# Order of row fetches and of row copies in a graph network kernel: four plain fetches ahead of the first that adds, and later row copies behind the first two tiles'

## The chip, the cores and the metric

The kernel runs on one core of a Trainium2 chip. The metric is the device time of one execution in microseconds (us). The kernel before takes 3490.05 us, the median of three runs (3488.29 to 3501.34).

The core's engines work side by side and meet at semaphores: TensorE (PE, matrix products into PSUM), VectorE (DVE, elementwise work and reductions), ScalarE (ACT, copies and activations), GpSimd (POOL, which here issues the indirect fetches) and SyncE (SP, which issues the plain DMAs). Each has its own list of instructions in an order fixed when the program is built.

## The reference

64 graphs of 256 nodes with 256 features go through four layers. Layers 0, 1 and 3 are of one kind, with different weights; layer 2 is an attention layer over a node's neighbours. The first kind, with the adjacency matrix used twice:

```python
pre_u = jnp.einsum('bud,dk->buk', h_t, W1[:d])
pre_v = jnp.einsum('bvd,dk->bvk', h_t, W1[d:])
hidden = jax.nn.relu(pre_u[:, :, None, :] + pre_v[:, None, :, :] + b1)
S = jax.nn.sigmoid(jnp.einsum('buvk,ko->buvo', hidden, W2)[..., 0] + b2[0])
a_t = jnp.einsum('buv,bud->bvd', S * A_a, h_t)
m_t = jnp.einsum('uv,bud->bvd', A_m, h_t) * h_t
z_t = beta1 * h_t + beta2 * (jnp.einsum('bvd,de->bve', a_t, Wa) + ba) + beta3 * (jnp.einsum('bvd,de->bve', m_t, Wm) + bm)
```

The score S(u, v) counts only where the adjacency matrix is not zero, that is on few pairs (u, v), the edges; they are the same for all graphs.

## The kernel before

The kernel counts the edges, and since there are few it runs `few`. It computes scores on edges alone. The edges are laid out in tiles of 128, one edge per partition; a tile holds, for two graphs, the sum pre_u[u] + pre_v[v] of each of its edges as 2 x 256 numbers. VectorE then takes relu, multiplies by W2's row and sums (`rated`, which writes `junk` and a column of `raw`); ScalarE turns `raw` into `val`, VectorE multiplies it with the edges' weights into `rm`, and TensorE spreads these products over the matrix `sa` (`spread`, the matmuls `ps<-rm,gu`).

There are two ways to gather the sum of a tile:

- A tile "made" by TensorE (`made`, line 757): ScalarE copies 64 rows of `pre_u` and 64 rows of `pre_v` into the tile `pre` (`rows_u` and `rows_v`, lines 826 and 834), and one matmul with a 0/1 matrix `pick` gathers and adds them in PSUM (`ga<-pre,pick`). `rows_u` writes two tiles in one copy of 64x1024 numbers, `rows_v` one tile per copy of 64x512. The list `FAST` has eight such tiles, or six in some blocks.
- A "fetched" tile (`got`, line 776): `pre_u` and `pre_v` are also written to tables in DRAM (`tableu`, `tablev`, by SP). POOL fetches one row per partition from `tableu` by index, and then one from `tablev` with an add onto the same tile (`fetch`, line 807; the DMA is at line 820 in the profile). There are eight such tiles in a block, or ten (`more`), and a half tile `left` for the rest.

A block is one layer of this kind for two graphs; there are 96 blocks. A block with eight fetched tiles has 18 fetches, one with ten has 22; 64 and 32 blocks have them. Graphs run on two sides, "a" and "b", which alternate: while the scores of one side's layer are computed, the other side goes through its matrix work (`beside`, line 904, which steps through both by written lists of counts). A pass in which both sides take two graphs through all layers recurs 16 times.

The order of the work around the change:

- POOL's order is the list `FETCHES`, a pair (tile, 0) for the plain fetch from `tableu` and (tile, 1) for the one that adds from `tablev`; tile -1 is `left`. Each fetch is set behind the one before it with `tc.issue_after`. An add waits until the plain fetch of its tile has landed. The first `AHEAD` = 6 are issued as soon as the tables' first halves are written (in `before`, line 642), the rest from `scores` (line 695).
- On the other engines the order is made by a scheduler when the program is built, within what `issue_after` demands. In `before`, the row copies of tiles 0 and 1 are emitted last (`rows_v(st, 4 - 4 * m, 2, 0)` with m = 1); in `made` those of tiles 2 and 3 (n = 0), 4 and 5 (n = 1), 6 and 7 (n = 2), set behind `past[-1]`, the last `val` of the block before.

Of the kernel before, what the change touches and what calls it, by code (L numbers as in the profile page):

```python
# [35 lines left out]
MORE = FAST[6:]  # L36
FIRST = 4

FETCHES = [(0, 0), (1, 0), (2, 0), (0, 1), (3, 0), (1, 1)]
FETCHES += [(-1, 0), (2, 1), (4, 0), (3, 1), (-1, 1), (5, 0), (6, 0), (4, 1), (7, 0), (5, 1), (6, 1), (7, 1)]  # L40
FETCHES_MORE = FETCHES[:-2] + [(8, 0), (6, 1), (9, 0), (7, 1), (8, 1), (9, 1)]

# [20 lines left out]
def blk(c):  # L63
    return slice(c * P, (c + 1) * P)
# [37 lines left out]
def adj_seq_kernel(ctx: ExitStack, tc: tile.TileContext, a: dict, out: bass.AP):  # L102
# [15 lines left out]
    tensor, vector, scalar = Noting(nc.tensor), Noting(nc.vector), Noting(nc.scalar)  # L118
# [379 lines left out]
    def few(stack):  # L498
# [139 lines left out]
        def more(st, l):  # L638

            return (st["side"], l) in (("a", LAST), ("b", GNN[1]))  # L640

        def before(st, l):

            hT = st["hT"]
            pu = one.tile([P, 2, 2, D], FP, tag="pu" + st["side"], name="pu")
            pv = one.tile([P, 2, 2, D], FP, tag="pv" + st["side"], name="pv")
            pre = one.tile([P, len(FAST), 2 * D], FP, tag="pre" + st["side"], name="pre")
            order = [(m, g) for m in range(2) for g in range(2)]
            if l == LAST:
                order = [(m, g) for g in range(2) for m in range(2)]  # L650

            beside = {LAST: [0, (0, 1), (0, 1), (0, 1)], GNN[1]: [0] + [(0, 1)] * 3, GNN[0]: [0, 0, (0, 2), (0, 1)]}[l]
            beside = dict(zip(order, beside))
            st["tables"] = [
                tables.tile([N, 2 * D], FP, tag="table" + t + st["side"], name="table" + t) for t in "uv"
            ]

            st["pu"], st["pv"], st["pre"] = pu, pv, pre
            if l != GNN[1]:
                st["own"] = one.tile([P, 2, 2, D], FP, tag="own", name="own")  # L660
            t = one.tile([P, FIRST, 2, D], FP, tag="fetched" + st["side"], name="fetched")
            st["fetched"] = [t[:, f] for f in range(FIRST)]
            for m, g in order:
                if l == LAST and (m, g) == (1, 0):
                    st["flip"](1)
                t = psum()
                for c in range(2):
                    mm(out=t, lhsT=hT[:, c, g, blk(m)], rhs=w1[l][:, c], start=c == 0, stop=c == 1)
                scalar.copy(pu[:, m, g, :], t[:, 0, :])
                vector.tensor_tensor(pv[:, m, g, :], t[:, 1, :], b1row[l], ALU.add)  # L670
                if g == 1:
                    for rows, x in zip(st["tables"], (pu, pv)):
                        nc.sync.dma_start(out=rows[blk(m)], in_=flat(x)[:, m])
                    if m == 0:
                        st["fetches"] = list(FETCHES_MORE if more(st, l) else FETCHES)

                        if numbered:
                            fetch(st, AHEAD)
                if l != GNN[1]:
                    vector.tensor_tensor(st["own"][:, m, g, :], t[:, 0, :], pv[:, m, g, :], ALU.add)  # L680
                if g == 1:
                    if m == 0:
                        rows_u(st, 0, 2, 0, 0)
                    rows_v(st, 4 - 4 * m, 2, 0)
                yield beside[(m, g)]
                if l == GNN[1] and (m, g) == (0, 1):
                    st["turn"](0)
                    yield 0, 1
                    st["turn"](1)
                    yield 0  # L690
            yield REST_OF_IT

            yield from mixed(st, l, later if past else None, (0,) if more(st, l) else (0, 1))

        def scores(st, l, placed):
# [33 lines left out]
            def tile_scores(t, k, m, i):  # L729
                col = BLOCKS + 16 * m + 4 * k + i  # L730
                both(t, col, col + 8)
# [18 lines left out]
            def itself(m):  # L750

                with stay(vector):
                    if l == GNN[1]:
                        vector.tensor_tensor(*(flat(t)[:, m] for t in (own, st["pu"], st["pv"])), ALU.add)
                    both(own[:, m], DIAGONAL + 2 * m, DIAGONAL + 2 * m + 1)

            def made():
                for n, (k, m, i) in enumerate(fast):
                    t = ga.tile([P, 2, D], FP, tag="ga", name="ga")
                    with stay(tensor):  # L760
                        mm(out=t, lhsT=pick[:, k, 4 * m + i, :], rhs=pre[:, n], start=True, stop=True)
                    tile_scores(t, k, m, i)
                    if 2 * n + 2 < len(fast):

                        with tc.issue_after(past[-1]) if past else nullcontext():
                            rows_u(st, 2 * n + 2, 2, *FAST[2 * n + 2][:2])
                            if n != 1:
                                rows_v(st, 2 * n + 2, 2, FAST[2 * n + 2][0])
                    if n in (1, 2) and not placed:
                        itself(n - 1)  # L770
                    count.append(n)
                    yield
                    if n == 2 and more(st, l):
                        yield from mixed(st, l, None, (1,), ga)
# [25 lines left out]
            def end():  # L800
                rated_all(LATE, 1)
                past.append(st["rated"].ins)

            made = made()
            return made, got(made), end

        def fetch(st, n):

            now, st["fetches"] = st["fetches"][:n], st["fetches"][n:]
            for f, x in now:  # L810
                rows = st["tables"][x]
                if f < 0:
                    to, ids = st["left"], (left_u, left_v)[x]
                    rows = rows.rearrange("n (g d) -> (n g) d", g=2)
                else:
                    to, ids = st["fetched"][f].rearrange("p g d -> p (g d)"), (ids_u, ids_v)[x][:, f : f + 1]
                    if f < FIRST:
                        rows = rows[blk(0)]
                with tc.issue_after(fetches[-1]) if fetches else nullcontext():
                    this = nc.gpsimd.indirect_dma_start(  # L820
                        out=to, out_offset=None, in_=rows, in_offset=bass.IndirectOffsetOnAxis(ap=ids, axis=0),
                        compute_op=(ALU.bypass, ALU.add)[x],
                    )
                fetches.append(this.ins)

        def rows_u(st, f, n, k, m):

            h = halves[k]
            scalar.copy(
                st["pre"][h, f : f + n],  # L830
                st["pu"][h, m].rearrange("p g d -> p (g d)").unsqueeze(1).to_broadcast([64, n, 2 * D]),
            )

        def rows_v(st, f, n, k):

            for n in range(f, f + n):
                i = FAST[n][2]
                scalar.copy(
                    st["pre"][halves[1 - k], n], st["pv"][halves[i % 2], i // 2].rearrange("p g d -> p (g d)")
                )  # L840
# [37 lines left out]
        def stream(side, starts):  # L878

            sts = [{"b": b, "side": side} for b in starts]  # L880
            load(sts[0])
            short = [before(sts[0], GNN[0])]
            for i, st in enumerate(sts):
                yield short, (st, GNN[0]), False
                yield [after(st, GNN[0]), before(st, GNN[1])], (st, GNN[1]), True
                yield [after(st, GNN[1]), attention(st), before(st, GNN[2])], (st, GNN[2]), False
                short = [after(st, GNN[2])]
                if i + 1 < len(sts):
                    load(sts[i + 1])
                    short = [halfway(after(st, GNN[2]), 4, before(sts[i + 1], GNN[0]), 2)]  # L890
            yield short, None, False
# [29 lines left out]
        past, numbered, fetches, later = [], [], [], []  # L921
# [119 lines left out]
```

## Time and profile before

| | us |
|---|---|
| median of the runs (lowest, highest) | 3490.05 (3488.29, 3501.34) |
| the profiled execution | 3499.89 |
| its span, first to last instruction | 3498.2 |
| mean granted TensorE clock | 0.993 |
| ScalarE, a copy of `pre_u` rows, two tiles | 1.044 |
| ScalarE, a copy of `pre_v` rows, one tile | 0.617 |
| POOL, issue of a plain fetch, of an adding fetch (mean) | 1.010, 1.579 |
| VectorE, one `junk` of a tile and graph | 0.418 |

The profile is of one execution. Its page gives each engine's busy time and share of the span, the instructions grouped by source line, engine and tile, and the idle time ahead of a group with what ended it. "PE ga <- ACT pre" means that TensorE's matmul into `ga` waited for ScalarE's write of `pre`. Nearly all instructions of PE, DVE and ACT carry line 79, since a helper records them; they are told apart by their tiles. Queries of the trace answer with the waits of an engine, its instructions in order of time, and the busy time in chosen stretches.

### The profile page before, as it was taken

How to read it: one execution, taken by the hardware profiler on the slowest of the kernel's cores; microseconds unless marked ns; L12 is line 12 of the kernel's file. 1: busy time of each engine (PE TensorE's matmuls, PEld its weight loads, DVE VectorE, ACT ScalarE, POOL GpSimd, SP SyncE). 2: the span in 40 equal slices, each digit the busy share in tenths (PEclk: the TensorE clock that was granted, in tenths of full speed). 3: DMA queues.
4: the chain of work that ended last, by engine and by line, in shares of the span. 5: the costliest groups of instructions: out<-in, count | busy, mean ns of one | idle time of the engine just before them, and what ended most of it. 6: DMA issues, size and time to landing. Idle time of an engine off the chain costs nothing.

```text
span 3498.2 us, 48226 instructions
## 1 busy us (share of the span) xinstructions
PE 3391.1 (97%) x14200; PEld 2079.5 (59%) x14200; DVE 2626.2 (75%) x10526; ACT 1554.0 (44%) x2833; POOL 2409.6 (69%) x1882
## 2 busy tenths in 40 slices
PE   6999999999999999999999999999999999999998
PEld 3566565665656556565665656556565565656655
DVE  5777777777777777777777777777777777777776
ACT  2444444444444444544444444444444444444442
POOL 3767767677776767677677776776767667676765
PEclk7999999999999999999999999999999999999999
DMA  5788787877878878788787878778788788787875
GB/s 146 164 181 187 166 204 163 188 174 172 199 168 193 179 169 191 172 191 176 174 192 165 197 168 184 178 167 198 165 190 176 173 191 171 190 178 175 190 166 125
DMA packets 289070, 620.81 MB, mean 177 GB/s; under 512 B 39072, under 2 KB 56352, under 8 KB 288800
## 3 DMA queue, kind: packets, MB, share of 16 engines
q0 software_dynamic: 204800, 461.49, 66.6%
q1 hardware_dynamic: 82416, 154.96, 12.6%
q8 instruction: 115, 1.88, 0.2%
q10 hardware_dynamic: 1584, 1.20, 0.1%
q14 instruction: 155, 1.27, 0.1%
HBM read 500.06 MB, written 117.44 MB: 177 GB/s over the span
## 4 chain that ended last, share of the span: by engine, by line
PE 62%; POOL 10%; DMA 10%; DVE 8%; issue 7%; ACT 3%; another core or an unknown queue 0%; POOLq 0%; ACTq 0%; SPq 0%; DVEq 0%
PE ps L79 48%; PE ga L79 13%; POOL fetched L820 9%; DMA fetched<-tablev,ids_v 6%; DVE junk L79 3%; DMA fetched<-tableu,ids_u 3%; ACT pre L79 2%; DVE rm L79 1%; POOL left L820 1%; DVE sa L79 1%; DMA tableu<-pu 1%; DVE own L79 1%; ACT val L79 1%; ACT pu L79 1%; DVE mT L79 0%
## 5 line engine op out<-in xcount | busy, mean ns | idle before, releaser
L820 POOL DMA_INDIRECT fetched<-tablev,ids_v x832 | 1313.7, 1579 | 415.3 <-issue 256.1
L820 POOL DMA_INDIRECT fetched<-tableu,ids_u x832 | 840.5, 1010 | 548.8 <-DMA tableu<-pu 285.4
L79 DVE SCALAR_TENSOR_TENSOR junk<-fetched,L_gnn_w2row 128x256 f32<-128x256 f32 x1664 | 642.4, 418 | 205.8 <-DMA fetched<-tablev,ids_v 203.7
L79 PE MATMUL ga<-pre,pick 128*128 128x512 f32 x1408 | 721.5, 607 | 36.0 <-ACT pre L79 24.6
L79 PE MATMUL ps<-L_gnn_w,hT 128*128 128x512 f32 x1536 | 706.7, 597 | 5.8 <-DMA hT<-in_xT_dram 5.8
L79 DVE SCALAR_TENSOR_TENSOR junk<-ga,L_gnn_w2row 128x256 f32<-128x256 f32 x1408 | 537.3, 419 | 110.6 <-PE ga L79 94.6
L79 PEld LDWEIGHTS ps<-L_gnn_w,hT 128*128 128x128 f32 x1536 | 279.7, 190 | 323.2 <-issue 296.3
L79 ACT COPY pre<-pv 64x512 f32<-64x512 f32 x704 | 434.1, 617 | 70.8 <-DVE pv L79 47.3
L79 ACT COPY pre<-pu 64x1024 f32<-64x1024 f32 x352 | 361.4, 1044 | 7.4
L79 PE MATMUL ps<-sa,h 128*128 128x256 f32 x1536 | 359.8, 380 | 4.7 <-DVE sa L79 4.7
L79 PEld LDWEIGHTS ps<-sa,h 128*128 128x128 f32 x1536 | 291.7, 190 | 114.4 <-issue 62.5
L79 PEld LDWEIGHTS ga<-pre,pick 128*128 128x128 f32 x1408 | 248.5, 190 | 183.6 <-issue 92.5
L79 ACT COPY pu<-ps 128x256 f32<-128x256 f32 x384 | 142.8, 372 | 478.2 <-PE ps L79 450.3
L79 ACT ACTIVATE hb<-hT,L_gnn_zbias,scas 128x512 f32<-128x512 f32 x128 | 97.4, 807 | 479.3 <-DVE hT L79 368.1
L79 DVE TENSOR_TENSOR rm<-gva,val 128x256 f32<-128x256 f32 x768 | 279.8, 419 | 28.7 <-ACT val L79 21.2
L79 PE MATMUL ps<-adj,h 128*128 128x256 f32 x1280 | 296.8, 383 | 3.9 <-issue 3.9
L79 PEld LDWEIGHTS ps<-adj,h 128*128 128x128 f32 x1280 | 241.6, 191 | 74.1 <-issue 40.0
L79 DVE TENSOR_TENSOR pv<-ps,L_gnn_b1row 128x256 f32<-128x256 f32 x384 | 161.3, 420 | 135.5 <-ACT pu L79 128.8
L79 PEld LDWEIGHTS ps<-rm,gu 128*64 128x64 f32 x3072 | 174.7, 137 | 144.5 <-issue 54.1
L79 PE MATMUL ps<-rm,gu 128*64 128x128 f32 x3072 | 218.8, 280 | 32.6 <-DVE rm L79 31.0
L79 ACT COPY aT<-ps 128x512 f32<-128x512 f32 x192 | 112.4, 585 | 299.7 <-PE ps L79 267.5
L79 PE MATMUL ps<-mT,L_gnn_Wm 128*128 128x512 f32 x512 | 240.6, 592 | 0.0
(153 smaller groups left out, 4239.6 us busy)
## 6 DMA issues: line engine op xcount, KB each, us to landing
tableu<-pu SPq DMA_DIRECT2D x192, 256.0 KB
tablev<-pv SPq DMA_DIRECT2D x192, 256.0 KB
hT<-in_xT_dram SPq DMA_DIRECT2D x32, 512.0 KB
h<-in_x_dram SPq DMA_DIRECT2D x64, 256.0 KB
out_dram<-h SPq DMA_DIRECT2D x64, 256.0 KB
fetched<-tableu,ids_u POOLq DMA_INDIRECT x832
fetched<-tablev,ids_v POOLq DMA_INDIRECT x832
L_gnn_w<-in_L_gnn_W_dram SPq DMA_DIRECT2D x6, 256.0 KB
```

Of the source, the lines that this page charges most:

```text
L79: self.last = getattr(self.engine, op)(*a, **k)
L820: this = nc.gpsimd.indirect_dma_start(out=to, out_offset=None, in_=rows, in_offset=bass.IndirectOffsetOnAxis(ap=ids, axis=0), compute_op=( ...
```

## The change

Two things. In the list of fetches, the plain fetch of tile 3 moves ahead of the first fetch that adds. And the row copies of tiles 2 and later are, besides the wait for the block before, also set behind the last row copy that `before` emitted, which is `pre_v`'s for tile 1; before, the scheduler was free to put the `pre_u` copy of tiles 2 and 3 ahead of those, and did so in the blocks of the last layer.

```diff
-FETCHES = [(0, 0), (1, 0), (2, 0), (0, 1), (3, 0), (1, 1)]
+FETCHES = [(0, 0), (1, 0), (2, 0), (3, 0), (0, 1), (1, 1)]
 FETCHES += [(-1, 0), (2, 1), (4, 0), (3, 1), (-1, 1), (5, 0), (6, 0), (4, 1), (7, 0), (5, 1), (6, 1), (7, 1)]
...
                     if m == 0:
                         rows_u(st, 0, 2, 0, 0)
                     rows_v(st, 4 - 4 * m, 2, 0)
+                    st["rows"] = scalar.last.ins
                 yield beside[(m, g)]
...
                     if 2 * n + 2 < len(fast):
 
-                        with tc.issue_after(past[-1]) if past else nullcontext():
+                        with tc.issue_after(past[-1]) if past else nullcontext(), tc.issue_after(st["rows"]):
                             rows_u(st, 2 * n + 2, 2, *FAST[2 * n + 2][:2])
                             if n != 1:
                                 rows_v(st, 2 * n + 2, 2, FAST[2 * n + 2][0])
```

In the order as built, ScalarE's list differs in the two blocks of the last layer of each pass (32 in all), and at the start: `pre<-pv` twice, `pre<-pu`, `pre<-pv` twice, where it was `pre<-pu` and then `pre<-pv` four times. TensorE's list differs in one place of each pass: eight `rm` matmuls, `ga`, eight `rm`, `ga` becomes three `rm`, `ga`, thirteen `rm`, `ga`. There VectorE's first addition into `sa` moves behind the two `junk` of that `ga`. POOL's list differs in every block by the moved fetch.

## The prediction

> **What bounds the kernel now.** I read the page's busy shares first, then TensorE's waits, then the timeline round each kind of wait.
>
> ```profile
> PE 3391.1 (97%) x14200; PEld 2079.5 (59%) x14200; DVE 2626.2 (75%) x10526; ACT 1554.0 (44%) x2833; POOL 2409.6 (69%) x1882
> ...
> PE ps L79 <- DVE rm L79: 31.0, 33, 6.0
> PE ga L79 <- ACT pre L79: 24.6, 30, 1.3
> ...
> POOL fetched L820 <- DMA fetched<-tableu,ids_u: 165.6, 149, 3.3
> ```
>
> TensorE works nearly all the time, so nothing can gain more than its gaps: 102.9 us over the timeline, 35.6 of them in the first 100 us, 11.2 in the last 30, hence 56 in the steady part (columns: us in total, times, longest). The page's chain gives a quarter of the span to POOL and DMA, but TensorE works beside them; what counts is where the chain comes back to TensorE late. That is in two waits: `ga` matmuls for ScalarE's row copies, `ps<-rm,gu` for VectorE's products. The third line is what the fetch edit touches: POOL standing before an add until the rows it adds to have landed.
>
> The timeline (start us, us, engine, what, count, idle before and what ended it), ScalarE and then TensorE, at the last layer of one side, and TensorE at that of the other:
>
> ```profile
> 1904.93 0.22 ACT L79 ACTIVATE val<-val 128x16 f32<-128x16 f32 x1
> 1905.17 1.04 ACT L79 COPY pre<-pu 64x1024 f32<-64x1024 f32 x1
> 1906.23 2.53 ACT L79 COPY pre<-pv 64x512 f32<-64x512 f32 x4
> ...
> 1904.80 1.09 PE L79 MATMUL ps<-rm,gu 128*64 128x128 f32 x16
> 1906.90 1.12 PE L79 MATMUL ga<-pre,pick 128*128 128x512 f32 x2 [1.01 <-ACT pre L79]
> 1907.96 1.09 PE L79 MATMUL ps<-rm,gu 128*64 128x128 f32 x16
> 1908.98 1.13 PE L79 MATMUL ga<-pre,pick 128*128 128x512 f32 x2
> ...
> 1949.59 1.12 PE L79 MATMUL ga<-pre,pick 128*128 128x512 f32 x2 [0.72 <-ACT pre L79]
> ```
>
> ScalarE copies `pre_u` rows of tiles 2 and 3 (1.04 us) and only then tile 0's own `pre_v` row, for which TensorE idles. Both places recur 16 times, once per pass of 213 us.
>
> POOL, VectorE, TensorE and (share of the 16 DMA engines, the last column but one) the stretch in which POOL waits:
>
> ```profile
> 2227.22 0.95 POOL L820 DMA_INDIRECT fetched<-tableu,ids_u  x1 [0.30 <-issue]
> 2231.37 1.81 POOL L820 DMA_INDIRECT fetched<-tablev,ids_v  x1 [3.20 <-DMA fetched<-tableu,ids_u]
> 2233.48 0.98 POOL L820 DMA_INDIRECT fetched<-tableu,ids_u  x1 [0.30 <-issue]
> ...
> 2229.91 0.43 DVE L79 SCALAR_TENSOR_TENSOR junk<-fetched,L_gnn_w2row 128x256 f32<-128x256 f32 x1 [1.56 <-DMA fetched<-tablev,ids_v]
> ...
> 2232.46 0.78 PE L79 MATMUL ps<-rm,gu 128*64 128x128 f32 x6 [2.09 <-DVE rm L79]
> ...
> 2228.40:2230.40 2.00, 1.98 (x19) 0.97 (x17) 0.49 (x3) 0.00 (x0) 0.00 (x0) 1.00 0.86 311
> 2230.40:2232.40 2.00, 0.00 (x0) 0.00 (x0) 1.38 (x6) 1.60 (x4) 1.03 (x1) 1.00 0.08 31
> ```
>
> While POOL waits, the DMA engines run dry (0.08). The VectorE line belongs to the block before, whose first add waited 2.95 us: its last add lands late, VectorE idles 1.56 us, then `rm`, and TensorE 2.09 us.
>
> [...] POOL's 3.20 us hold up every later fetch. [...]
>
> **Part 1, ScalarE, first place (16 times).** No instruction is added; the copy `pre<-pu` of tiles 2 and 3 moves behind the two `pre<-pv` of tiles 0 and 1. Tile 0's row then runs from 1905.17 (VectorE finished its source `pv` at 1905.02) to 1905.79; TensorE starts 0.05 later, as now: 1905.84 for 1906.90, 1.06 earlier. But the compiled order also moves this `ga`: it now stands behind 3 instead of 8 `rm` matmuls, with 13 instead of 8 behind it. Five of 0.107 us each (start to start in the timeline; a matmul has two records, so x16 is eight) come after it, 0.53. Net 1.06 − 0.53 = 0.53, times 16 = **8.5 us**. The second eight need `rm` products done at 1906.94, before TensorE reaches them at about 1907.4: hidden. VectorE's first `sa` addition moves behind two `junk` of tile 0; I get the second `sa` done at 1909.26, TensorE asking at 1909.4: hidden by 0.14 us, and at worst the 0.53 is lost. Tiles 2 and 3 are complete at the same time as now.
>
> **Part 1, second place (16 times).** Same swap, TensorE's order unchanged. The 16 waits (0.31 to 1.30, three of them put to "issue") sum to 8.5 us; each but one (1.30) is under the 1.04 us by which the copy comes earlier. Gain 8.5 − 0.3 = **8.2 us**. TensorE next meets `rm`, of which the later half is done at 1949.62 and wanted at about 1950: hidden, narrowly.
>
> **Part 2, POOL.** Before the first add there are now four plain fetches. The fourth passes that add; its 0.98 us plus 0.30 issue fill the wait. Per block POOL gains the smaller of 1.28 and the add's wait in excess of 0.30. Over the 96 blocks that wait averages 1.70 us in the 64 blocks with 18 fetches and 1.20 in the 32 with 22, so 0.91 us per block, and 1.26 in the 33 that start without a pause. Everything after the second add is issued that much sooner, over the whole block. The second add needs tile 1's rows, issued 1.28 after tile 0's: no new wait. The reused semaphore for which the moved fetch now waits is of a DMA eight issues back, some 12 us, against 5 to 8 us from issue to use where VectorE waits: hidden.
>
> Where does it reach TensorE? 23 of its waits on `rm` (19.2 us) follow VectorE's wait for a landed add by under 9 us. Taking for each the smaller of the wait and its block's POOL gain, I get 13.6 us; the last block adds 1.26 at the end, where TensorE waits 6.0 us: **14.9 us**. The other `rm` waits, mostly 0.43 us behind an activation, stay.
>
> Its unknown: the first add is issued 1.28 minus the excess later where the excess is smaller (up to 0.6 in most long blocks, those with 22 fetches), and its data follow one more fetch. A fetch costs the engines 66.6% of 3498.2 us over 1664 + 96 full fetches = 1.32 us; so it lands 0 to 1.9 later. I take 1. VectorE waits for tile 0 at once only in long blocks, and there it waits again about 2.5 us for tile 1, which comes sooner: hidden.
>
> **Sum.** 8.5 + 8.2 + 14.9 = 31.6. The gains overlap: what TensorE saves at the second place makes it earlier at the next `rm` wait, whose fetches started before. I take 85%, **27 us**. The profiled execution, 3499.89 us (span 3498.2), would be 3473; it lies 9.8 over the median 3490.05, so 3463 for the median.
>
> **Rivals.**
> A: ScalarE's part alone pays, the fetches being hidden or held by the DMA engines, which are 0.9 to 1.0 busy late in many blocks. For it: adds' data queue there. Against: the dry 2 us. 8.5 + 8.2 = 17, so 3473.
> B: almost nothing: `ga` behind three `rm` costs its gain, VectorE (75% busy overall, all of some 5 us stretches) is late instead. 0 to 8 us, say 3486.
> C, slower: the first add lands too late. It decides once the delay exceeds the 2.5 us that VectorE idles before tile 1 in the 32 long blocks; each us beyond costs up to 32. With part 2's gain gone, it needs 17/32 = 0.5 us more to end slower at all; two adds in a row that cost 4 us of delay would give 3490 − 17 + 1.5 × 32 = 3521. Against it: my bound is 1.9, and adds already follow each other three in a row at each block's end, where they are used 5 to 8 us after issue.
> That the change does nothing is out: the compiled order shows both moves.
>
> **Numbers.** Both parts 0.57 (3444 to 3471), A 0.20, B 0.14, C 0.09. 0.5% of 3490, 17.5 us, is about what a measurement of this kernel can tell. A lies on that bound and is halved: faster 0.57 + 0.10 = 0.67; same 0.10 + 0.14 = 0.24; slower 0.09. Range: 3445 (45 of the steady 56 us of gaps, should waits that I didn't count close too) to 3487 (B), leaving out C and the tails.
>
> **What would show it.** `PE ga <- ACT pre` falls from 24.6 to under 10 us, at the first place about 0.55 per wait; POOL's `fetched <- DMA fetched<-tableu` from 165.6 to about 80; `PE ps <- DVE rm` from 31 to about 17. Wrong if VectorE's wait for `tablev` (203.7 us) grows, if `ps<-sa,h` starts to wait, or if POOL's gain only lengthens its wait for the tables.

## The result, and the profile after

The changed kernel took 3602.56 us, the median of four runs (3596.70 to 3612.65), against 3491.45 for the kernel before beside it: a ratio of 1.0318, with a 95% interval of 1.0293 to 1.0342. It is slower by 111 us where 27 us less had been forecast. The profiled execution took 3603.28 us, its span 3601.6. Measured again with other runs beside it, the same program was once 2.0% slower and twice 0.9% faster; that is the main finding, and the experiments below turn on it.

The page of the kernel after, busy time of each engine:

```profile
PE 3441.3 (96%) x14200; PEld 2102.7 (58%) x14200; DVE 2622.5 (73%) x10526; ACT 1551.6 (43%) x2833; POOL 2416.4 (67%) x1882
```

TensorE does the same 14200 matmul records, but is busy 50.2 us longer and idle 53.2 us longer (span less busy: 160.3 against 107.1). The waits of the kernel after (who waits for what: us in total, times, longest):

```profile
POOL fetched L821 <- DMA tableu<-pu: 485.4, 68, 12.9
...
PE ps L79 <- DVE sa L79: 88.7, 46, 3.3
...
POOL fetched L821 <- DMA fetched<-tableu,ids_u: 56.1, 56, 3.0
...
DVE junk L79 <- DMA fetched<-tablev,ids_v: 36.7, 41, 2.3
...
PE ps L79 <- issue: 17.0, 17, 3.0
...
PE ps L79 <- DVE rm L79: 10.7, 10, 7.0
...
PE ga L79 <- ACT pre L79: 6.4, 16, 0.4
```

Everything that the change aimed at has fallen: POOL's wait for the rows it adds to from 165.6 to 56.1 us, VectorE's wait for landed adds from 203.7 to 36.7, TensorE's waits for `rm` from 31.0 to 10.7 and for ScalarE's copies from 24.6 to 6.4. Part of the fall comes from TensorE being later with everything else: in a profile of the same program at 3470 us, shown further below, these four waits are 122.0, 171.4, 26.4 and 6.7 us. In their place stand two others. POOL waits 485.4 us for the tables, 286.0 before; with VectorE's wait for landed adds down to 36.7 us, that is not what holds TensorE up. And TensorE's matmuls `ps<-sa,h` wait for VectorE's additions into `sa`; before, that was 4.7 us in five waits.

Where it happens is seen in the timeline of the kernel after, at the first place (last layer of side a; start us, us, engine, what, count, idle before and what ended it). ScalarE, TensorE, VectorE and POOL, one after the other:

```profile
642.62 1.04 ACT L79 COPY pre<-pu 64x1024 f32<-64x1024 f32 x1
643.66 1.25 ACT L79 COPY pre<-pv 64x512 f32<-64x512 f32 x2
...
642.12 1.12 PE L79 MATMUL ga<-pre,pick 128*128 128x512 f32 x2 [0.39 <-ACT pre L79]
643.18 1.74 PE L79 MATMUL ps<-rm,gu 128*64 128x128 f32 x26
644.85 1.12 PE L79 MATMUL ga<-pre,pick 128*128 128x512 f32 x2
645.81 0.59 PE L79 MATMUL ps<-sa,h 128*128 128x256 f32 x2
649.12 1.65 PE L79 MATMUL ps<-sa,h 128*128 128x256 f32 x5 [2.71 <-DVE sa L79]
...
644.08 0.69 DVE L79 TENSOR_TENSOR sa<-sa,ps 128x512 f32<-128x512 f32 x1
648.38 0.69 DVE L79 TENSOR_TENSOR sa<-sa,ps 128x512 f32<-128x512 f32 x1 [3.61 <-remote]
...
643.03 1.01 POOL L821 DMA_INDIRECT fetched<-tableu,ids_u  x1 [0.30 <-issue]
644.35 0.94 POOL L821 DMA_INDIRECT fetched<-tableu,ids_u  x1 [0.30 <-issue]
645.59 1.56 POOL L821 DMA_INDIRECT fetched<-tablev,ids_v  x1 [0.30 <-issue]
```

The edits have done their work. ScalarE's copies of tiles 2 and 3 now follow those of tiles 0 and 1, `ga` waits 0.39 us where it waited 1.01, and POOL goes from its fourth plain fetch into the first add with 0.30 us between. Then: the last of the thirteen `rm` matmuls ends, by its record, at 643.18 + 1.74 = 644.92. VectorE has nothing else to do and stands before its second addition into `sa`, which needs those matmuls and nothing more. It starts at 648.38, 3.46 us later; the trace names no releaser ("remote"). Meanwhile TensorE has run into `ps<-sa,h`: the first matmul needs only the first half of `sa`, the second needs the other half and waits 2.71 us for it. VectorE waits for TensorE's report, and TensorE for VectorE.

"Report" is here the semaphore event by which VectorE learns that the matmuls are done. The trace has the end of the matmul's record and, 3.46 us later, the start of the addition, and names no releaser; so it can't tell whether the matmul ended late or only its report came late. On another occasion (run e3_after below) the same addition of the same program starts 0.04 us behind that end, as the next timeline shows, TensorE and VectorE at the same place of the same pass:

```profile
625.89 1.74 PE L79 MATMUL ps<-rm,gu 128*64 128x128 f32 x26
627.56 1.13 PE L79 MATMUL ga<-pre,pick 128*128 128x512 f32 x2
628.52 2.75 PE L79 MATMUL ps<-sa,h 128*128 128x256 f32 x12
...
626.79 0.69 DVE L79 TENSOR_TENSOR sa<-sa,ps 128x512 f32<-128x512 f32 x1
627.67 0.69 DVE L79 TENSOR_TENSOR sa<-sa,ps 128x512 f32<-128x512 f32 x1 [0.19 <-PE ps L79]
```

With the start of `rm` as zero, the first addition comes at 0.90 us in both. The second comes at 1.78 us here and at 5.20 us there. Nothing in the program differs.

A late report costs twice, which the windows of the kernel after show (us of the stretch, then busy time and count of PE, PEld, DVE, ACT and POOL, the granted TensorE clock, the share of the DMA engines, GB/s):

```profile
646.00:648.00 2.00, 0.41 (x2) 0.00 (x1) 0.00 (x0) 0.00 (x0) 1.57 (x2) 1.00 0.58 174
...
650.00:652.00 2.00, 2.00 (x7) 1.55 (x6) 1.73 (x11) 0.59 (x1) 1.70 (x2) 0.51 0.82 152
```

First TensorE, VectorE and ScalarE stand still. Then TensorE works at half clock: from 650.03 on, 0.91 us behind the end of the 2.71 us wait, the granted clock is 0.50 for 3.41 us, and the records of `ps<-sa,h` start 0.43 us apart instead of 0.22. Of the 42 gaps of TensorE over 1.5 us behind the first 100 us of this profile, 24 have a half-clock stretch that begins between the start of the gap and 3.5 us behind its end, the shortest of these gaps being 1.56 us long; the other 18, of 1.55 to 3.18 us, have none. The changed kernel has 28 half-clock stretches here and 8 in e3_after, at mean granted clocks of 0.982 and 0.991.

The two spans of this one program, 3601.6 and 3470.4 us, differ by 131.2. TensorE's idle time is 160.3 against 73.9, 86.4 more: its waits `ps<-sa,h` for VectorE are 88.7 against none, those put to "issue" 17.0 against 3.5, and those for `rm` 10.7 against 26.4, so 88.7 + 13.5 − 15.7 = 86.5. Its busy time is 3441.3 against 3396.5, 44.8 more. The clock's loss, estimated from the mean granted clocks as (1 − 0.982) × 3601.6 = 64.8 against (1 − 0.991) × 3470.4 = 31.2, accounts for about 34 of that; what makes up the other 11 stays open.

### The profile page after: what moved, and what is told of

It reads as the page before. It is cut to its first block, busy times and chain, and to the rows that moved or that the text cites. A ratio compares the mean times of both kernels' runs of the same rounds, so it can differ in the third digit from the quotient of the medians.

```text
span 3601.6 us, 48226 instructions
## 1 busy us (share of the span) xinstructions
PE 3441.3 (96%) x14200; PEld 2102.7 (58%) x14200; DVE 2622.5 (73%) x10526; ACT 1551.6 (43%) x2833; POOL 2416.4 (67%) x1882
## 4 chain that ended last, share of the span: by engine, by line
PE 86%; DVE 5%; another core or an unknown queue 2%; ACT 2%; issue 2%; POOL 1%; DMA 0%; POOLq 0%; DVEq 0%; ACTq 0%
PE ps L79 69%; PE ga L79 17%; DVE junk L79 2%; DVE sa L79 2%; ACT pre L79 1%; DVE rm L79 1%; POOL fetched L821 1%; ACT val L79 0%; ACT pu L79 0%; DMA fetched<-tablev,ids_v 0%; DVE own L79 0%; DVE pv L79 0%; DMA fetched<-tableu,ids_u 0%; ACT logits L79 0%
## 5 line engine op out<-in xcount | busy, mean ns | idle before, releaser
L79 DVE SCALAR_TENSOR_TENSOR junk<-fetched,L_gnn_w2row 128x256 f32<-128x256 f32 x1664 | 638.3, 418 | 37.1 <-DMA fetched<-tablev,ids_v 36.7
L79 PE MATMUL ps<-sa,h 128*128 128x256 f32 x1536 | 407.7, 410 | 99.9 <-DVE sa L79 88.7
L79 PEld LDWEIGHTS ps<-sa,h 128*128 128x128 f32 x1536 | 310.2, 205 | 241.9 <-DVE sa L79 118.6
L79 DVE TENSOR_TENSOR rm<-gva,val 128x256 f32<-128x256 f32 x768 | 279.9, 419 | 28.2 <-ACT val L79 15.7
L79 DVE TENSOR_TENSOR hT<-hb,ps 128x512 f32<-128x512 f32 x128 | 87.9, 687 | 241.4 <-PE ps L79 241.3
L79 DVE TENSOR_TENSOR sa<-sa,ps 128x512 f32<-128x512 f32 x192 | 129.4, 684 | 182.8 <-remote 89.7
```

The lines of the kernel that those rows point to most:

```text
L79: self.last = getattr(self.engine, op)(*a, **k)
```

## Experiments

All medians are in us. The ratio is the record's own estimate from the single runs, and differs from the ratio of the medians by up to 0.0014. "Late" counts, of the 96 second additions into `sa` (one per block), those which start more than 1.5 us after the recorded end of their last `rm` matmul.

| run | what | median | before beside it | ratio (95%) | late | `ps<-sa,h` for VectorE |
|---|---|---|---|---|---|---|
| first | change | 3602.56 | 3491.45 | 1.0318 (1.0293–1.0342) | 51 | 88.7 |
| e1_fetch | fetch order alone | 3478.10 | 3495.73 | 0.9953 (0.9936–0.9969) | 0 | 0 |
| e1_rows | ScalarE's order alone | 3493.31 | 3495.73 | 0.9998 (0.9988–1.0008) | 0 | 0 |
| e1_two | two plain fetches ahead | 3585.81 | 3495.73 | 1.0257 (1.0240–1.0275) | 0 | 0 |
| e1_paced | fetch order, paced | 3508.59 | 3495.73 | 1.0035 (1.0017–1.0053) | 0 | 0 |
| e2_after | change | 3569.10 | 3496.48 | 1.0200 (1.0174–1.0227) | 49 | 85.5 |
| e2_before | before | 3494.08 | 3496.48 | – | 3 | 2.9 |
| e2_rows_a | change, rows on side a only | 3565.50 | 3496.48 | 1.0211 (1.0182–1.0240) | 45 | 63.9 |
| e2_rows_b | change, rows on side b only | 3565.67 | 3496.48 | 1.0186 (1.0160–1.0212) | 49 | 78.5 |
| e3_after | change | 3467.98 | 3496.74 | 0.9912 (0.9894–0.9930) | 0 | 0 |
| e3_fetch | fetch order alone | 3478.99 | 3496.74 | 0.9948 (0.9931–0.9965) | 0 | 0 |
| e3_rows | ScalarE's order alone | 3495.67 | 3496.74 | 0.9992 (0.9982–1.0002) | 0 | 0 |
| e3_paced | fetch order, paced | 3509.72 | 3496.74 | 1.0035 (1.0020–1.0051) | 0 | 0 |
| e4_both_paced | change, paced | 3507.25 | 3503.50 | 1.0012 (1.0003–1.0021) | 1 | 0 |
| e4_rows | ScalarE's order alone | 3501.35 | 3503.50 | 1.0000 (0.9987–1.0013) | 11 | 11.8 |
| e5_fetch | fetch order alone | 3475.87 | 3495.27 | 0.9937 (0.9918–0.9956) | 0 | 0 |
| e5_after | change | 3469.11 | 3495.27 | 0.9913 (0.9894–0.9933) | 0 | 0 |
| e5_mend | change, more work before `sa` | 3543.04 | 3495.27 | 1.0132 (1.0109–1.0154) | 0 | 0 |
| e6_fetch | fetch order alone | 3601.63 | 3503.74 | 1.0267 (1.0233–1.0300) | 50 | 81.5 |

Runs whose names begin alike (e1, e2, ...) were measured on one chip, side by side. The groups fall into two kinds. In e1, e3 and e5 no report is late, whatever the kernel. In the first measurement, e2, e4 and e6 some are late; in the first measurement and e2 that holds for the kernel before too (four and three), in e4 and e6 it was not profiled. The first kind I call prompt, the second late. All profiles of the kernel before are of late occasions. Where waits of a prompt run are set against its waits below, the two occasions differ as well; its own two profiles have 31.0 and 26.3 us for `rm`, 24.6 and 22.6 for `pre`.

### Which part costs: the first group

The first trace suggested theory 1: plain fetches that follow one another closely delay TensorE's reports. Theory 2 put the cost down to ScalarE's part, which moves a `ga` and VectorE's additions; theory 3 was the prediction's rival C, the first add landing late.

```diff
 # e1_fetch: the kernel before, with the new list
+FETCHES = [(0, 0), (1, 0), (2, 0), (3, 0), (0, 1), (1, 1)]
```

> The fetch order alone, ScalarE's copies as before. Theory 1 (three or four plain fetches in a row delay the moment at which TensorE's finished rm matmuls are reported to VectorE; VectorE's second addition into sa is late, TensorE stands before ps<-sa,h and then works at half clock): 3560 to 3620 us, TensorE's wait ps<-sa,h for VectorE 60 us or more, against 4.7 before. Theory 2 (the cost comes from ScalarE's part: three rm, ga, thirteen rm at the first place): 3470 to 3490 us, that wait under 10 us. Theory 3 (the first add lands late): VectorE's wait for tablev over 204 us.

```diff
 # e1_rows: the change, with the old list
+FETCHES = [(0, 0), (1, 0), (2, 0), (0, 1), (3, 0), (1, 1)]
```

> ScalarE's order alone, the fetches as before. Theory 1: 3465 to 3485 us, the wait ps<-sa,h under 15 us, ga for ScalarE's pre under 10 us. Theory 2: 3580 to 3610 us, with the wait ps<-sa,h once per pass at the first place at least.

```diff
 # e1_two: the kernel before, two plain fetches ahead of the first add
+FETCHES = [(0, 0), (1, 0), (0, 1), (2, 0), (1, 1), (3, 0)]
```

> The kernel before with two plain fetches ahead of the first add instead of three: (0,0) (1,0) (0,1) (2,0) (1,1) (3,0). Theory 1: the late reports become rarer than before (the wait ps<-sa,h at most 5 us, no addition into sa later than 1 us after its last rm matmul while VectorE idles), POOL waits longer for the rows it adds to (165.6 us to 250 or more), the time 3490 to 3530 us. Theories 2 and 3: no view on the wait; the time by POOL alone, the same range.

```diff
 # e1_paced: e1_fetch, and in fetch() ahead of the issue
+                if (f, x) == (3, 0):
+                    for _ in range(2):
+                        with tc.issue_after(fetches[-1]):
+                            fetches.append(nc.gpsimd.memset(st["fetched"][3], 0.0).ins)
```

> The fetch order of the changed kernel alone, but POOL is kept busy about 1.3 us ahead of the fourth plain fetch (it clears that tile twice, which the fetch overwrites). Theory 1, by the rate of the plain fetches: the wait ps<-sa,h falls to under 25 us and the time to 3490 to 3530 us. If what counts is only that four plain fetches stand ahead of the first add, at whatever rate, it stays at 3560 to 3620 us with 60 us or more.

None of them explains the 111 us from here: neither part alone was slower, and no addition was late in any of the four. The waits of e1_fetch, then of e1_rows:

```profile
PE ga L79 <- ACT pre L79: 24.7, 32, 1.9
...
PE ps L79 <- DVE rm L79: 16.6, 23, 6.0
```

```profile
PE ps L79 <- DVE rm L79: 43.9, 43, 5.7
...
PE ga L79 <- ACT pre L79: 7.0, 16, 0.7
```

The fetch order alone gains 17.6 us by the medians, and the wait for `rm` falls by 14.4. ScalarE's order alone takes 17.6 us from the wait for `pre`, and the wait for `rm` grows by 12.9: nothing is left. e1_two shows how much hangs on what stands ahead of the first add: with two, three and four plain fetches the kernel takes 3586, 3496 and 3478 us. The waits of e1_two:

```profile
PE ps L79 <- DVE rm L79: 87.5, 50, 5.8
PE ga L79 <- ACT pre L79: 40.4, 40, 1.8
```

I had expected 3490 to 3530 from POOL's longer wait (it rose to 341.9 us). TensorE's two waits grew by 56.5 and 15.8 us, and its mean clock fell to 0.983 (0.993 in the first profile of the kernel before). The pause of e1_paced costs 13 us against the kernel before, where the same order without it gains 17.6.

Two new theories stood then: the parts hurt only together (theory 4), or what was slow in the first measurement is a property of the occasion (theory 5).

### Only together, or only sometimes: the second and third groups

e2_after and e2_before are the changed kernel and the kernel before, with no edit.

> The changed kernel once more, beside the kernels of this group. Theory 4 (the two parts hurt only together): 3580 to 3615 us, ps<-sa,h waiting for VectorE 60 us or more, and the second addition into sa over 2.5 us behind its last rm matmul in most passes, as in its first profile. Theory 5 (the late reports are not a property of the program, but of the occasion on which it was measured): 3455 to 3490 us, that wait under 10 us and the second addition 0.1 us behind.

> The kernel before, profiled beside them. Its first profile had four waits ps<-sa,h of 0.5 to 1.8 us, each behind a late report of an rm matmul. Theory 5: none of these here, and a span 3 to 10 us shorter. Theory 4: a few again, at the same places of other passes.

```diff
 # e2_rows_a, and e2_rows_b with "b"
-... tc.issue_after(st["rows"]):
+... tc.issue_after(st["rows"]) if st["side"] == "a" else nullcontext():
```

> The new fetch order, with ScalarE's new order only in the last layer of side a (the first place, where TensorE's list becomes three rm, ga, thirteen rm). Theory 4: slower than the fetch order alone (3478) if the hurt comes from TensorE's moved ga, 3530 to 3600; 3470 to 3485 if it comes from the second place. Theory 5: 3465 to 3480 us.

> The new fetch order, with ScalarE's new order only in the last layer of side b (the second place, where TensorE's list is as before). Theory 4: the reverse of the run with side a, 3530 to 3600 if the hurt comes from here, else 3465 to 3480. Theory 5: 3465 to 3480 us.

The change was slow again, and with ScalarE's part in only one of the two places it was as slow. That looked like theory 4, but the kernel before had late reports too, three of 96, where the four kernels of the first group, so near to it, had none. So the third group put the change and its parts side by side; e3_fetch, e3_rows and e3_paced are the kernels of the first group, e3_after is the changed kernel.

> The changed kernel in one group with its two parts alone. On a chip like that of the first group (all of TensorE's reports prompt, none of its semaphore events missing from the trace), theory 5 expects 3455 to 3480 us and no wait ps<-sa,h; theory 4 (the parts hurt only together) 3560 to 3615 on any chip. On a chip like that of the second group both expect 3560 to 3615.

> The fetch order alone. Theory 4: 3470 to 3485 us on any chip. Theory 5 with theory 1 (on some chips TensorE's reports are late while plain fetches follow one another closely): 3470 to 3485 on a chip with prompt reports; 3550 to 3610 on one with late reports, with ps<-sa,h waiting 50 us or more and 40 or more of the 96 second additions into sa over 1.5 us late.

> ScalarE's order alone. Theory 4: 3485 to 3500 us on any chip. Theory 5 with theory 1: the same on a chip with prompt reports; on one with late reports 3485 to 3510, with a few late additions as in the kernel before (under 15 over 1.5 us), because its fetches are as before.

> The new fetch order with about 1.3 us of POOL work ahead of the fourth plain fetch, ScalarE as before: 3508.6 us and no late report in the first group. Theory 4: again 3500 to 3520. Theory 5 with theory 1: again so on a chip with prompt reports; on one with late reports between the kernel before and the fetch order alone, under 25 second additions over 1.5 us late, since the fetches are further apart.

Theory 4 fell: the program that took 3603 us takes 3468, and no report is late. Each of its parts does what it did in the first group. The two kinds of occasion can be told apart without looking at any addition. On late ones semaphore events are missing from the trace: of the 11984 updates by TensorE, VectorE and ScalarE of the changed kernel 9882 are there, against 11983 in e3_after. In all nine late profiles 82 to 87% are there, in all eleven prompt ones at least 99.9%. It is not the chip alone: groups e1 and e4 ran on the same one. What the occasions differ in stays open. One suspect was not tested: every time here comes with a recorded span, and the missing events are missing from that recording, so no run shows whether the late reports would come without it.

### What makes a report late: the other groups

In seven late profiles of either fetch order (the first two, the four of e2, and e6_fetch), I took the share of the 16 DMA engines that packets of plain fetches held from 0.2 us before to 0.8 us after the end of each block's last `rm` matmul. Under 0.4, 20 of 364 second additions are over 1 us late; from 0.4 up, 254 of 308. Packets of adding fetches go the other way: in the first two profiles 58 of 133 additions are over 1 us late where these packets held under 0.4, and 1 of 59 from 0.4 up. In ten prompt profiles (all but e5_mend) 460 of 960 additions fall into the upper class too, and none is late.

The pooled count hides that the two orders differ. In the upper class 245 of 252 are late with the new fetch order, but 9 of 56 with the old one. So a high share of plain packets does not make a report late by itself. A pause of POOL separates the cases better. Take for each addition the block whose fetches began last before the end of its `rm`, and POOL's longest pause ahead of that block's first add. In the two profiles of the kernel before, 12 of 27 additions without a pause over 0.6 us are over 1 us late, and none of 165 with one. In e4_rows, with the same fetch order, it is 12 of 14, and 1 of 82; in the five late profiles of the new order 262 of 409, and none of 71. So it shows within one and the same program. And the fourth plain fetch fills just this pause: in the first measurement 84 of 96 blocks have it in the kernel before, 12 in the changed one. On prompt occasions none of 462 additions without it is late. All of that is correlation; the next runs put a pause back.

e4_both_paced is the changed kernel with the four lines of e1_paced, e4_rows is e1_rows.

> Both parts of the change, with about 1.3 us of POOL work ahead of the fourth plain fetch. On a chip with late reports: if the plain fetches that follow one another closely cause them, under 30 of the 96 second additions into sa are over 1.5 us late (49 and 51 in the changed kernel there) and the time is 3500 to 3550 us; if ScalarE's part or the mere order causes them, 45 or more and 3565 to 3610. On a chip with prompt reports: none late, 3490 to 3510 us.

> ScalarE's part alone, fetches as before. On a chip with late reports: under 15 second additions over 1.5 us late and 3485 to 3510 us if the plain fetches cause them; 40 or more and 3550 or more if ScalarE's part does. On a chip with prompt reports: none, 3485 to 3500 us, as twice before.

The occasion was of the late kind (10264 of 11984 events in e4_rows). With a pause ahead of the fourth plain fetch one addition is late instead of 51 or 49 (seven more are 1.1 to 1.4 us late), and the line `ps<-sa,h` for VectorE is gone from TensorE's waits. TensorE, VectorE and POOL at the first place, in the same pass as above:

```profile
631.27 1.74 PE L79 MATMUL ps<-rm,gu 128*64 128x128 f32 x26
...
633.05 0.69 DVE L79 TENSOR_TENSOR sa<-sa,ps 128x512 f32<-128x512 f32 x1 [0.19 <-PE ps L79]
...
631.13 1.01 POOL L825 DMA_INDIRECT fetched<-tableu,ids_u  x1 [0.30 <-issue]
632.14 1.12 POOL L823 MEMSET fetched<- 128x512 f32 x2
633.53 0.95 POOL L825 DMA_INDIRECT fetched<-tableu,ids_u  x1 [0.27 <-POOL fetched L823]
```

The second addition starts 0.04 us behind the end of `rm` (631.27 + 1.74 = 633.01). With the fetches as before and ScalarE's part alone there are 11 late additions, and the time is that of the kernel before. So ScalarE's part is not the cause; the fetch order without a pause is what brings the late reports, so far as one run with the pause shows. The changed kernel itself was not run on this occasion (its 51 and 49 are from two others), and the pause also moves the fourth fetch and all behind it later, so that spacing and moment are not told apart.

e5_fetch and e5_after are again the fetch order alone and the change.

> The fetch order alone, beside the whole change. With late reports on this occasion: 3545 to 3600 us and 40 or more of the 96 second additions over 1.5 us late, if the closely following plain fetches are the cause by themselves; under 20 and 3475 to 3510 if ScalarE's part is needed too. With prompt reports: 3470 to 3490 us, as twice before.

> The whole change again. With late reports: 3560 to 3610 us, 45 or more late. With prompt reports: 3460 to 3480 us, none late.

```diff
 # e5_mend: the change, and at the end of spread()
-            yield 1 if l == GNN[1] else 2
+            yield 3 if l == GNN[1] else 4
```

> The whole change, with two more of the made tiles stepped between the rm matmuls and ps<-sa,h, so that TensorE has 0.4 to 1.7 us more of other work before it needs the second addition. With late reports: the reports stay as late (40 or more over 1.5 us), but the wait ps<-sa,h falls from 85 us to 50 or less and the time to 3510 to 3560 us. With prompt reports: no wait to save, 3465 to 3500 us, by whether the earlier tiles find their row copies done.

This occasion was prompt, so the mend had no late report to hide. It missed its range: moving the tiles forward made other matmuls wait (47.2 us for ScalarE's `logits`, which cost 0.2 in e5_after) and lost 74 us against the change. Whether more work between `rm` and `sa` would pay on a late occasion was not seen. The last run is the fetch order alone once more.

> The fetch order alone, on another occasion. With late reports: 3545 to 3600 us and 40 or more of the 96 second additions over 1.5 us late, if the closely following plain fetches are the cause by themselves; under 20 and 3475 to 3510 us if ScalarE's part is needed too. With prompt reports: 3470 to 3490 us, as on three occasions before, and nothing is told apart.

This time the occasion was late. The waits of e6_fetch:

```profile
PE ps L79 <- DVE sa L79: 81.5, 57, 3.5
PE ga L79 <- ACT pre L79: 17.3, 19, 1.0
```

The fetch order alone, 0.5 to 0.6% faster on three prompt occasions, costs 2.7% here, as much as the whole change in its first measurement. The new fetch order is enough by itself to bring the late reports on such an occasion; a pause in it took nearly all of them away in the one run that tried. No kernel here beats the kernel before on both kinds of occasion: on prompt ones the change is the best, on late ones nothing gains.

## Why the prediction was right or wrong

**Part 2, POOL, 14.9 us: near in size on prompt occasions.** The fetch order alone gains 17.6, 17.8 and 19.4 us there, and TensorE's waits for `rm` are 16.6 to 20.7 us, against 31.0 in the profile before. POOL's wait for the rows it adds to is 113.0 us in e1_fetch, not about 80, and most of what it saves there it waits longer for the tables (326.7 us against 286.0). Landed adds still come sooner: VectorE waits 157.2 us for them, 203.7 before.

**Part 1, ScalarE, 8.5 + 8.2 us: the waits right, the gain wrong by itself.** `ga` for `pre` fell to about 7 us in e1_rows, e3_rows, e3_after and e5_after, and the first place waits 0.39 us in the timeline shown, near the 0.53 to 0.55 worked out. But alone the part gains 2.4 and 1.1 us, within the uncertainty, because TensorE then meets `rm` earlier and waits 12.9 us more there than in the profile before. Rival A, 3473 by ScalarE's part alone, is thereby out. On top of the fetch order the part gains 11.0 us (3478.99 to 3467.98) and 6.8 us (3475.87 to 3469.11).

**The sum, 27 us: met on prompt occasions, in part by luck.** There the change gains 28.8 and 26.2 us, with 3468 and 3469 against the 3463 forecast. But ScalarE's part, put at 16.7, brings 11.0 and 6.8, and the fetches, put at 14.9, bring 17.8 and 19.4: the errors cancel. The waits of e3_after:

```profile
PE ps L79 <- DVE rm L79: 26.4, 28, 5.7
...
PE ga L79 <- ACT pre L79: 6.7, 16, 0.8
```

The wait for `rm` is 26.4 us (27.0 in e5_after), not about 17: what TensorE gains at `pre` it loses in part at `rm`. The overlap was assumed to shrink both parts alike; in truth ScalarE's part pays only on top of the fetch order.

**The step that failed: Part 2 took POOL's pause ahead of the first add as free to fill.** Of the fourth plain fetch it says that "its 0.98 us plus 0.30 issue fill the wait", and books a gain of up to 1.28 us per block. What an unbroken row of fetches does to TensorE's reports to VectorE was put at nothing, without a reason. On late occasions the runs show in its place 88.7 us of waits `ps<-sa,h` in the first measurement, and 81.5 with the fetch order alone, where ScalarE's part is absent; the time is 3603 and 3602 us.

The prediction looked at this handover only in Part 1, at one place: "hidden by 0.14 us, and at worst the 0.53 is lost." On prompt occasions the first clause holds: the second addition is done at 627.67 + 0.69 = 628.36, and TensorE asks for it after its first `ps<-sa,h` matmul, some 0.43 us behind 628.52. The second clause was no bound. It took the time from the end of `rm` to the start of the addition as fixed, because the profile showed it so at that place. In the first measurement that time was 3.46 us and TensorE lost 2.71 us there. Of its 46 waits 16, with 41.3 us, lie at this place; the other 30, with about 47 us and up to 3.3 us each, lie at places where TensorE's own order had not changed. Often it went on at half clock, as in 24 of the 42 gaps counted above.

The profile before held the sign. Its timeline, pass of 1904 us, second place, TensorE, VectorE and POOL:

```profile
1954.36 0.59 PE L79 MATMUL ps<-sa,h 128*128 128x256 f32 x2
1956.77 1.56 PE L79 MATMUL ps<-sa,h 128*128 128x256 f32 x6 [1.82 <-DVE sa L79]
...
1956.03 0.69 DVE L79 TENSOR_TENSOR sa<-sa,ps 128x512 f32<-128x512 f32 x1 [2.94 <-remote]
...
1950.76 0.94 POOL L820 DMA_INDIRECT fetched<-tableu,ids_u  x1 [0.31 <-issue]
1952.01 1.56 POOL L820 DMA_INDIRECT fetched<-tablev,ids_v  x1 [0.30 <-issue]
```

VectorE is idle for 2.94 us before an addition whose matmuls had ended at 1952.61. In this pass POOL went from the third plain fetch into the first add with 0.30 us between. So it is, with 0.5 us at most, in four of the 16 passes at this place, and in these the addition starts 1.1 to 3.4 us behind its matmuls; in the other twelve POOL pauses for 1.0 to 1.7 us, and it starts 0.41 us behind at most. There were five waits `ps<-sa,h` for VectorE, 4.7 us in all, too little to be looked at by their sum. This one asked why finished matmuls were not taken up, and the change takes the pause out of most blocks.

**Rival C, the first add landing late: fell.** VectorE's wait for `tablev` sank in every run of the new order that was not paced (157.2 us in e1_fetch, 36.7 in the first profile). It was the only rival on the slow side, and the chance of 0.09 for slower came from it alone. Of the signs named at the end, "if `ps<-sa,h` starts to wait" came. POOL's longer wait for the tables came too, but not alone: on prompt occasions it rose to 322 to 327 us, and the change still paid.

## What to carry to other kernels

A handover between two engines that is hidden by tenths of a microsecond is only as safe as the longest gap that the trace shows for it anywhere, so look up the rare long waits of a group, not only its sum. A pause that looks like waste can be what another handover lives on (1 late report of 96 with a pause put back, 51 and 49 without): before filling it, compare in the profile the blocks that have it with those that don't. Here, on some occasions, fetches in an unbroken row went with reports of matmuls that came up to 4.9 us late. When a result contradicts a well supported sum, measure the same program again beside its parts before explaining it by the program.

## What was not expected of the hardware

TensorE's report of finished matmuls, judged by the start of the second addition into `sa`, came 0.04 to 0.07 us behind their recorded end in 67 of 96 blocks of the first profile of the kernel before, and up to 4.9 us behind it in that of the changed kernel: over 1 us in 53 of the 85 cases in which POOL issued four plain fetches and the first add without a pause over 0.6 us, and in none of the 11 with one. VectorE's and ScalarE's own reports in the same trace came within 0.012 us of the last end before them in 99 of 100 cases, of those that the trace has. It appears on some occasions and not on others, on one chip in both ways, together with 13 to 18% of semaphore events missing from the trace. What distinguishes these occasions, whether and by which path fetches hold up a report, and whether the recording has a part in it, no run here tells. Behind an idle stretch of TensorE of 2.71 us, the granted clock was 0.50 for 3.41 us, from 0.91 us after it.
